# Q, K and V projections of a graph attention layer as 15 instead of 18 block products

## The chip, the cores and the metric

The kernel runs on one core of one Trainium2 chip. The metric is the device time of one execution in microseconds, as the median of several runs. The kernel before takes 3695.78 us (three runs, 3694.63 to 3697.33).

## The reference

For 128 graphs of 128 nodes and 768 features, everything in float32:

```python
h = jnp.maximum(_layernorm(x, axis=-1), 0.0)
q = _split_heads(h @ Wq + bq)      # 12 heads of 64
k = _split_heads(h @ Wk + bk)
v = _split_heads(h @ Wv + bv)
scores = jnp.einsum('bhqd,bhkd->bhqk', q, k) / jnp.sqrt(HD)
scores = scores + beta * adj_e
scores = jnp.where(adj_e > 0, scores, -9e15)
out = jnp.einsum('bhqk,bhkd->bhqd', softmax(scores), v)
x = x + out                        # heads joined again
```

## The kernel before

The function `direct` works on groups `G` of four graphs, 32 groups in all, so one group is a block of 512 rows. The 768 features are six chunks of 128 (`c` for the summed dimension, `oc` for the output dimension; an output chunk of 128 is two heads). The three weight matrices are loaded once, on the ACT queue, and stay in SBUF.

Per group: `load_x` brings x on the SP queue. `norm` (L125 to L138) normalises one graph: two `bn_stats` (L131), an aggregate and an add on DVE, a power on POOL (L137), and the scaling `xn` on DVE (L138). `to_hT` (L140 to L146) turns one feature chunk of the four graphs with four PE transposes `pt` and writes it through a ReLU on ACT as `hT`, 128 x 512. `make_bias` builds the transposed mask and bias from adj with DVE, POOL, four transposes `pb` and an ACT copy.

`project_qk(G, oc)` is 6 matmuls for q and 6 for k, each with 128x128 weights as the stationary operand and 512 columns of `hT` as the moving one, summed in one PSUM bank (`pwq`, `pwk`, L187); DVE reads q out (L191), ACT reads k out (L193). `project_v` takes `hT` as the stationary operand and 384 columns of `wv` as the moving one, 8 PSUM tiles of 6 matmuls (`pv`, L175), read out by DVE (L178). `scores` is 8 matmuls per output chunk (`sc`, L202), then a DVE operation (L207) and an exponential on ACT (L208) for each of two heads. `attend` is 8 matmuls (`av`, L217), and then sm, rs, seen, o and seen on DVE and an add into x on POOL (L229). The store of a whole group follows its last add.

In float32 each matmul is two records in the trace, each a weight load and a pass over the moving columns; "pass" below is one such record. A transpose is one.

The source order is: for each `oc`, `project_qk`, then (at `oc` 0) `project_v`, then `attend` of the chunk before, then `scores`; `norm` of the next group stands at `oc` 0 to 3, `to_hT` at 4 and 5. A planner puts each engine's instructions into a fixed order before the run: it follows source order where its own estimate says that an operand and a buffer are there, and takes something later in the source where they aren't. On the chip each engine runs its list in that order.

Of the kernel before, what the change touches and what calls it, by code (L numbers as in the profile page):

```python
# [59 lines left out]

@with_exitstack
def direct(ctx, tc, x, adj, wq, bq, wk, bk, wv, bv, beta, out, bad):

# [46 lines left out]
    bk_c = const.tile([P, NC], F32, name="bk_c")  # L110
    with nc.allow_non_contiguous_dma(reason="two biases of one row each"):
        nc.scalar.dma_start(bq_c, bq.rearrange("(c p) -> p c", p=P))
        nc.scalar.dma_start(bk_c, bk.rearrange("(c p) -> p c", p=P))
    bv_b = const.tile([P, D], F32, name="bv_b")
    nc.scalar.dma_start(bv_b, bv[None, :].to_broadcast([P, D]))
    w_sb = {}
    for name, src in (("wq", wq), ("wk", wk), ("wv", wv)):
        w_sb[name] = const.tile([P, NC, D], F32, name=name)
        for c in range(NC):
            nc.scalar.dma_start(w_sb[name][:, c, :], src[c * P:(c + 1) * P, :])  # L120
    vs = [const.tile([P, GRP, HEADS, VE], F32, name=f"v{i}") for i in range(2)]
    for v in vs:
        nc.gpsimd.memset(v[:, :, :, HD:VE], 1.0)

    def norm(G, g):  # L125
        if g == 0:
            xn[G] = big.tile([P, GRP, D], F32, tag="xn", name=f"xn_{G}", bufs=1)
        xg = xs[G][:, g, :]
        st = stat.tile([P, 2, nc.vector.BN_STATS_DIM], F32, tag="st", name=f"st_{G}_{g}")
        for s in range(2):  # L130
            nc.vector.bn_stats(st[:, s, :], xg[:, s * VH:(s + 1) * VH])  # L131
# [6 lines left out]
        nc.vector.tensor_scalar(xn[G][:, g, :], xg, mv[:, 0:1], rstd, op0=ALU.subtract, op1=ALU.mult)  # L138

    def to_hT(G, c):  # L140
        if c == 0:
            hT[G] = big.tile([P, NC, W], F32, tag="hT", name=f"hT_{G}")
        p = psum.tile([P, W], F32, tag="mm", name=f"pt_{G}_{c}", bufs=4)
        for g in range(GRP):
            nc.tensor.transpose(p[:, g * N:(g + 1) * N], xn[G][:, g, c * P:(c + 1) * P], ident)  # L145
        nc.scalar.activation(hT[G][:, c, :], p, AF.Relu)  # L146

    def make_bias(G):
        a = adjs[G]
        b = work.tile([P, GRP, N], F32, tag="b", name=f"b_{G}", bufs=1)  # L150
        nc.vector.tensor_scalar(b, a, beta_c, BIAS_CAP, op0=ALU.mult, op1=ALU.min)
        kp = work.tile([P, GRP, N], U8, tag="kp", name=f"kp_{G}", bufs=1)
        nc.vector.tensor_scalar(kp, a, 0.0, None, op0=ALU.is_gt)
        bm = stat.tile([P, GRP], F32, tag="bm", name=f"bm_{G}", bufs=1)
        b2 = work.tile([P, GRP, N], F32, tag="b2", name=f"b2_{G}", bufs=1)
        nc.gpsimd.tensor_tensor(b2, b, b, ALU.mult)
        nc.vector.tensor_reduce(bm, b2, AX.X, ALU.max)
        nc.vector.tensor_tensor(seen_b, seen_b, bm, ALU.max)
        nb = work.tile([P, GRP, N], F32, tag="nb", name=f"nb_{G}", bufs=1)
        nc.gpsimd.memset(nb, MASKED)  # L160
        nc.vector.copy_predicated(nb, kp, b)
        p = psum.tile([P, GRP, N], F32, tag="mm", name=f"pb_{G}", bufs=4)
        for g in range(GRP):
            nc.tensor.transpose(p[:, g, :], nb[:, g, :], ident)  # L164
        biasT[G] = big.tile([P, GRP, N], F32, tag="biasT", name=f"biasT_{G}")
        nc.scalar.copy(biasT[G], p)

    def project_v(G):
        v = vs[G % 2]
        HH = HEADS // 2  # L170
        for g in range(GRP):
            for s in range(2):
                p = psum.tile([P, VH], F32, tag="mm", name=f"pv_{G}_{g}_{s}", bufs=4)
                for c in range(NC):
                    nc.tensor.matmul(p, hT[G][:, c, g * N:(g + 1) * N],  # L175
                                     w_sb["wv"][:, c, s * VH:(s + 1) * VH],
                                     start=(c == 0), stop=(c == NC - 1))
                nc.vector.tensor_add(v[:, g, s * HH:(s + 1) * HH, 0:HD],  # L178
                                     p.rearrange("p (h d) -> p h d", d=HD),
                                     bv_b[:, s * VH:(s + 1) * VH].rearrange("p (h d) -> p h d", d=HD))  # L180

    def project_qk(G, oc):
        got = []
        for name in ("wq", "wk"):
            p = psum.tile([P, W], F32, tag="mm", name=f"p{name}_{G}_{oc}", bufs=4)
            for c in range(NC):
                nc.tensor.matmul(p, w_sb[name][:, c, oc * P:(oc + 1) * P], hT[G][:, c, :],  # L187
                                 start=(c == 0), stop=(c == NC - 1))
            t = work.tile([P, W], F32, tag=name, name=f"{name}T_{G}_{oc}", bufs=2)
            if name == "wq":  # L190
                nc.vector.tensor_scalar(t, p, bq_c[:, oc:oc + 1], SCALE, op0=ALU.add, op1=ALU.mult)  # L191
            else:
                nc.scalar.activation(t, p, AF.Identity, bias=bk_c[:, oc:oc + 1])  # L193
            got.append(t)
        return got

    def scores(G, oc, qT, kT):
        ps = [psum.tile([P, GRP, N], F32, tag="sc", name=f"sc_{G}_{oc}_{j}") for j in range(2)]
        for g in range(GRP):
            for j in range(2):  # L200
                r = slice(j * HD, (j + 1) * HD)
                nc.tensor.matmul(ps[j][:, g, :], kT[r, g * N:(g + 1) * N], qT[r, g * N:(g + 1) * N],  # L202
                                 start=True, stop=True)
        es = []
        for j in range(2):
            e = work.tile([P, GRP, N], F32, tag="e", name=f"e_{G}_{oc}_{j}")
            nc.vector.scalar_tensor_tensor(e, ps[j], SCORE_CAP, biasT[G], op0=ALU.min, op1=ALU.add)  # L207
            nc.scalar.activation(e, e, AF.Exp)  # L208
            es.append(e)
        return es  # L210

    def attend(G, oc, es):
        pa = psum.tile([P, 2, 512], F32, tag="av", name=f"av_{G}_{oc}", bufs=1)
        for g in range(GRP):
            for j in range(2):
                at = ((g % 2) * 2 + j) * VE
                nc.tensor.matmul(pa[:, g // 2, at:at + VE], es[j][:, g, :], vs[G % 2][:, g, 2 * oc + j, :],  # L217
                                 start=True, stop=True)
        got = pa[:, :, 0:4 * VE].rearrange("p a (b e) -> p a b e", e=VE)
        sm = stat.tile([P, 2, 4, 1], F32, tag="sm", name=f"sm_{G}_{oc}")  # L220
        nc.vector.tensor_scalar(sm, got[:, :, :, HD:VE], TINY, None, op0=ALU.max)  # L221
        rs = stat.tile([P, 2, 4, 1], F32, tag="rs", name=f"rs_{G}_{oc}")
        nc.vector.reciprocal(rs, sm)
        o = work.tile([P, 2, 4, HD], F32, tag="o", name=f"o_{G}_{oc}", bufs=2)
        nc.vector.tensor_mul(o, got[:, :, :, 0:HD], rs.to_broadcast([P, 2, 4, HD]))  # L225
        for i, t in enumerate((sm, rs)):
            nc.vector.tensor_tensor(seen[:, i, :], seen[:, i, :], t.rearrange("p a b e -> p (a b e)"), ALU.max)  # L227
        xo = xs[G][:, :, oc * P:(oc + 1) * P]
# [7 lines left out]
    for c in range(NC):  # L236
        to_hT(0, c)
# [3 lines left out]
    for G in range(NG):  # L241
        for oc in range(NC):
            qT, kT = project_qk(G, oc)
            if oc == 0:
                project_v(G)
# [158 lines left out]
```

## Time and profile before

| | us |
|---|---|
| median of three runs | 3695.78 |
| the profiled execution | 3694.58 |
| its span, from the first to the last instruction | 3692.5 |
| PE busy in it | 3648.3 |
| DVE busy | 1036.9 |
| ACT busy | 474.3 |
| POOL busy | 367.7 |

The busy time of an engine is the time in which at least one of its instructions runs. PE (matmul passes) and PEld (weight loads) are two rows of one engine, and run beside each other. A group of the steady part repeats every 113.85 us, so that the stretch between two `pv` of successive groups stands for all of them.

### The profile page before, as it was taken

How to read it: one execution, taken by the hardware profiler on the slowest of the kernel's cores; microseconds unless marked ns; L12 is line 12 of the kernel's file. 1: busy time of each engine (PE TensorE's matmuls, PEld its weight loads, DVE VectorE, ACT ScalarE, POOL GpSimd, SP SyncE). 2: the span in 40 equal slices, each digit the busy share in tenths (PEclk: the TensorE clock that was granted, in tenths of full speed). 3: DMA queues.
4: the chain of work that ended last, by engine and by line, in shares of the span. 5: the costliest groups of instructions: out<-in, count | busy, mean ns of one | idle time of the engine just before them, and what ended most of it. 6: DMA issues, size and time to landing. Idle time of an engine off the chain costs nothing.

```text
span 3692.5 us, 34646 instructions
## 1 busy us (share of the span) xinstructions
PE 3648.3 (99%) x14722; PEld 2100.4 (57%) x14722; DVE 1036.9 (28%) x2598; ACT 474.3 (13%) x801; POOL 367.7 (10%) x396
## 2 busy tenths in 40 slices
PE   6999999999999999999999999999999999999998
PEld 3555555555555555555555555555555555555554
DVE  3232222322222323223222232222332222322222
ACT  0111111111111101111101111111110111101111
POOL 1011000110001101011100011000110001100000
PEclk9999999999999999999999999999999999999999
DMA  4011010110101101001011011010110100100000
GB/s 144 3 38 38 34 38 3 38 38 35 38 3 38 38 35 38 21 21 38 35 37 38 3 38 38 35 38 3 38 38 35 38 17 24 38 35 35 18 1 35
DMA packets 55294, 118.80 MB, mean 32 GB/s; under 512 B 3552, under 2 KB 19936, under 8 KB 55136
## 3 DMA queue, kind: packets, MB, share of 16 engines
q1 hardware_dynamic: 50688, 109.06, 8.2%
q10 hardware_dynamic: 4448, 7.48, 0.6%
q8 instruction: 118, 1.93, 0.2%
q14 instruction: 40, 0.33, 0.0%
HBM read 66.20 MB, written 50.33 MB: 32 GB/s over the span
## 4 chain that ended last, share of the span: by engine, by line
PE 99%; DMA 1%; DVE 0%; ACT 0%; POOL 0%; issue 0%; ACTq 0%; DVEq 0%; POOLq 0%
PE pwq L187 27%; PE pv L175 27%; PE pwk L187 27%; PE av L217 9%; PE sc L202 6%; PE pt L145 3%; PE pb L164 0%; DMA adj<-in_adj_dram 0%; DMA x<-in_x_dram 0%; DVE xn L138 0%; POOL rstd L137 0%; DVE st L131 0%; DVE o L225 0%; ACT L146 0%; ACT e L208 0%
## 5 line engine op out<-in xcount | busy, mean ns | idle before, releaser
L187 PE MATMUL pwq<-hT,wq 128*128 128x512 f32 x2304 | 1033.9, 598 | 0.0
L187 PE MATMUL pwk<-hT,wk 128*128 128x512 f32 x2304 | 1020.1, 592 | 0.0
L175 PE MATMUL pv<-wv,hT 128*128 128x384 f32 x3072 | 996.0, 486 | 0.0
L175 PEld LDWEIGHTS pv<-wv,hT 128*128 128x128 f32 x3072 | 583.7, 190 | 413.9 <-issue 15.1
L187 PEld LDWEIGHTS pwk<-hT,wk 128*128 128x128 f32 x2304 | 437.8, 190 | 551.0 <-issue 543.4
L187 PEld LDWEIGHTS pwq<-hT,wq 128*128 128x128 f32 x2304 | 422.4, 190 | 474.9 <-issue 451.6
L229 POOL TENSOR_TENSOR x<-x,o 128x512 f32<-128x512 f32 x192 | 244.9, 1276 | 3125.7 <-DVE seen L227 3125.7
L178 DVE TENSOR_TENSOR v<-pv,bv_b 128x384 f32<-128x384 f32 x256 | 143.0, 559 | 1005.0 <-PE pv L175 1005.0
L217 PEld LDWEIGHTS av<-v,e 128*128 128x128 f32 x3072 | 373.2, 192 | 86.8 <-issue 76.5
L208 ACT ACTIVATE e<-e 128x512 f32<-128x512 f32 x384 | 231.2, 627 | 1382.5 <-DVE e L207 1381.6
L217 PE MATMUL av<-v,e 128*128 128x65 f32 x3072 | 364.2, 272 | 1.7 <-ACT e L208 1.7
L193 ACT ACTIVATE wkT<-pwk,bk_c 128x512 f32<-128x512 f32 x192 | 132.0, 687 | 1623.2 <-PE pwk L187 1623.2
L221 DVE TENSOR_SCALAR sm<-av 128x8 f32<-128x8 f32 x192 | 32.0, 167 | 1009.2 <-PE av L217 1009.2
L191 DVE TENSOR_SCALAR wqT<-pwq,bq_c 128x512 f32<-128x512 f32 x192 | 142.6, 743 | 526.9 <-PE pwq L187 526.9
L207 DVE SCALAR_TENSOR_TENSOR e<-sc,biasT 128x512 f32<-128x512 f32 x384 | 246.3, 683 | 0.8 <-PE sc L202 0.6
L202 PE MATMUL sc<-wqT,wkT 64*128 64x128 f32 x3072 | 223.1, 285 | 0.0
L202 PEld LDWEIGHTS sc<-wqT,wkT 64*128 64x128 f32 x3072 | 186.3, 187 | 13.5 <-issue 0.5
L131 DVE BATCH_NORM_STATS2 st<-x 128x6 f32<-128x384 f32 x256 | 132.0, 534 | 13.4 <-DMA x<-in_x_dram 13.1
L225 DVE TENSOR_TENSOR o<-av,rs 128x512 f32<-128x512 f32 x192 | 132.8, 692 | 9.4
L145 PE MATMUL pt<-ident,xn 128*128 128x128 f32 x768 | 101.2, 282 | 30.9 <-DVE xn L138 15.7
L146 ACT ACTIVATE hT<-pt 128x512 f32<-128x512 f32 x192 | 106.9, 595 | 165.2 <-PE pt L145 165.0
L145 PEld LDWEIGHTS pt<-ident,xn 128*128 128x128 f32 x768 | 84.5, 143 | 40.1 <-DVE xn L138 16.9
(37 smaller groups left out, 474.1 us busy)
## 6 DMA issues: line engine op xcount, KB each, us to landing
x<-in_x_dram SPq DMA_DIRECT2D x32, 1536.0 KB, 6.6
out_dram<-x SPq DMA_DIRECT2D x32, 1536.0 KB, 5.4
adj<-in_adj_dram SPq DMA_DIRECT2D x32, 256.0 KB, 2.8
wq<-in_L_gnn_Wq_dram ACTq DMA_DIRECT2D x6, 384.0 KB, 7.4
wk<-in_L_gnn_Wk_dram ACTq DMA_DIRECT2D x6, 384.0 KB, 10.4
wv<-in_L_gnn_Wv_dram ACTq DMA_DIRECT2D x6, 384.0 KB, 6.2
bv_b<-in_L_gnn_bv_dram ACTq DMA_DIRECT2D x1, 384.0 KB, 9.1
beta_c<-in_L_gnn_beta_dram ACTq DMA_DIRECT2D x1, 0.5 KB, 3.7
```

The costliest lines, as they stand in the source:

```text
L131: nc.vector.bn_stats(st[:, s, :], xg[:, s * VH:(s + 1) * VH])
L145: nc.tensor.transpose(p[:, g * N:(g + 1) * N], xn[G][:, g, c * P:(c + 1) * P], ident)
L175: nc.tensor.matmul(p, hT[G][:, c, g * N:(g + 1) * N], w_sb["wv"][:, c, s * VH:(s + 1) * VH], start=(c == 0), stop=(c == NC - 1))
L178: nc.vector.tensor_add(v[:, g, s * HH:(s + 1) * HH, 0:HD], p.rearrange("p (h d) -> p h d", d=HD), bv_b[:, s * VH:(s + 1) * VH].rearrange(" ...
L187: nc.tensor.matmul(p, w_sb[name][:, c, oc * P:(oc + 1) * P], hT[G][:, c, :], start=(c == 0), stop=(c == NC - 1))
L191: nc.vector.tensor_scalar(t, p, bq_c[:, oc:oc + 1], SCALE, op0=ALU.add, op1=ALU.mult)
L202: nc.tensor.matmul(ps[j][:, g, :], kT[r, g * N:(g + 1) * N], qT[r, g * N:(g + 1) * N], start=True, stop=True)
L207: nc.vector.scalar_tensor_tensor(e, ps[j], SCORE_CAP, biasT[G], op0=ALU.min, op1=ALU.add)
L208: nc.scalar.activation(e, e, AF.Exp)
L217: nc.tensor.matmul(pa[:, g // 2, at:at + VE], es[j][:, g, :], vs[G % 2][:, g, 2 * oc + j, :], start=True, stop=True)
L225: nc.vector.tensor_mul(o, got[:, :, :, 0:HD], rs.to_broadcast([P, 2, 4, HD]))
L229: nc.gpsimd.tensor_add(xo, xo, o.rearrange("p a (b j) d -> p (a b) (j d)", j=2))
```

## The change

The projections of a group become a product of block matrices. The activations are 2 x 3 blocks of 256 x 256 (two graphs each by two feature chunks, `A00` to `A12`), the weights 3 x 3 blocks of 256 x 256 (`B00` to `B22`); a "slice" of 768 output columns has six output blocks. There are three slices: `qk0` (q and k of the first three output chunks, side by side), `v`, and `qk1` (q and k of the last three). 18 block products would give a slice; the list `PRODUCTS` gives it with 15, each of one activation block or sum of blocks (`S..`) and one weight block or sum of blocks (`T..`).

A block product is 4 matmuls with 256 moving columns (before: 512 for q and k, 384 for v). Products of one chain (a, b, c or d) are added to the same PSUM bank, which always holds the running sum; after most products that sum is added to, or taken from, one output block in SBUF. In a qk slice the first use of each of the six output blocks is two ACT operations (one each for q and k, with the bias), the other ten are DVE operations of 128 x 512 from PSUM into SBUF; in the v slice all 16 are DVE operations. A chain's next product writes into the bank that the last use has to have read.

The sums of weight blocks are made once and stay in SBUF, 15 operations for each slice on DVE and POOL, from weights loaded block by block (for qk: 18 loads of 128 KB for each slice). The sums of activation blocks are 11 operations per group (7 on DVE, 4 on POOL), each with one buffer. The x tiles are loaded graph by graph and normalised in place; the x of the residual add is loaded a second time in pieces of 128 x 512 (`xo`), and the output is stored in such pieces. `attend` works in two halves. The scale of the scores moves into the exponential. `attention` and `slice_of` put scores and attend of half a group between the products of the slice after: the first half in `qk1` of the same group, the second in `qk0` of the next one. After the last slice the second half of the last group is left.

```diff
+PRODUCTS = (
+    ("S9", "T9", "c", (((1, 1), -1),)),
+    ("A10", "T12", "a", (((1, 0), -1),)),
+    ("S10", "T10", "b", (((1, 0), 1),)),
+    ("S2", "T2", "c", (((0, 1), -1),)),
+    ("S8", "B12", "d", (((1, 1), -1), ((1, 2), 1))),
+    ("S6", "T6", "a", (((0, 0), -1),)),
+    ("S3", "B01", "c", (((0, 2), -1),)),
+    ("S7", "T7", "b", (((0, 0), 1),)),
+    ("A12", "T4", "d", (((1, 0), -1),)),
+    ("S14", "B21", "c", (((0, 1), 1),)),
+    ("S0", "T0", "a", (((0, 2), 1),)),
+    ("A01", "T13", "b", (((0, 1), 1),)),
+    ("A02", "T1", "c", (((0, 0), 1),)),
+    ("S5", "B22", "a", (((1, 2), 1),)),
+    ("S11", "T11", "b", (((1, 1), 1),)),
+)
...
+    psum = ctx.enter_context(tc.tile_pool(name="psum", bufs=4, space=bass.MemoryType.PSUM))
...
+    def load_x(G, g):
+        xg[G, g] = work.tile([P, D], F32, tag="x", name=f"x_{G}_{g}")
+        nc.sync.dma_start(xg[G, g], x[G * GRP + g])
...
+    def sum_acts(G, n):
+        name, a, b, sign = SUMS_A[n]
+        t = work.tile([P, 2, H2], F32, tag=name, name=f"{name}_{G}", bufs=1)
+        e = nc.gpsimd if n % 3 == 1 else nc.vector
+        e.tensor_tensor(t, A[G, a], A[G, b], ALU.add if sign > 0 else ALU.subtract)
...
+    def product(G, sl, n):
+        an, bn, chain, uses = PRODUCTS[n]
+        first = all(p[2] != chain for p in PRODUCTS[:n])
+        if first:
+            banks[chain] = psum.tile([P, 2, H2], F32, tag="mm", name=f"p{chain}_{G}_{sl}")
+        p = banks[chain]
+        a, b = A[G, an], wt[sl, bn]
+        for i in range(2):
+            for c in range(2):
+                if sl == "v":
+                    lhs, rhs = a[:, c, i * N:(i + 1) * N], b[:, c, :]
+                else:
+                    lhs, rhs = b[:, c, i * P:(i + 1) * P], a[:, c, :]
+                nc.tensor.matmul(p[:, i, :], lhs, rhs, start=(first and i == 0 and c == 0), stop=(c == 1),
+                                 skip_group_check=True)
+        for (r, j), sign in uses:
...
+            elif key not in qk:
+                t = qk[key] = work.tile([P, 2, H2], F32, tag="qk", name=f"{sl}_{G}_{r}_{j}", bufs=10)
+                oc = j + 3 * int(sl[2])
+                for i in range(2):
+                    nc.scalar.activation(t[:, i, :], p[:, i, :], AF.Identity, bias=bqk[:, i, oc:oc + 1],
+                                         scale=float(sign))
+            else:
+                t = qk[key]
+                nc.vector.tensor_tensor(t, t, p, ALU.add if sign > 0 else ALU.subtract)
...
+    def attention(G, u):
+        todo = {}
+        for i in range(3):
+            todo.setdefault(1 + 4 * i, []).append(lambda oc=3 * u + i: scores(G, oc))
+            todo.setdefault(5 + 4 * i, []).insert(0, lambda oc=3 * u + i: attend(G, oc))
+        return todo
+
+    def slice_of(G, sl, todo):
+        for n in range(len(PRODUCTS)):
+            product(G, sl, n)
+            for f in todo.get(n, ()):
+                f()
...
     for G in range(NG):
+        todo = attention(G - 1, 1) if G else {}
+        if not G:
+            load_weights("v")
+            for n in range(len(SUMS_B)):
+                todo.setdefault(n, []).append(lambda n=n: sum_weights("v", n))
+        slice_of(G, "qk0", todo)
+        todo = {}
+        if not G:
+            load_weights("qk1")
+            for n in range(len(SUMS_B)):
+                todo.setdefault(n, []).append(lambda n=n: sum_weights("qk1", n))
+        if G + 1 < NG:
+            for g in range(GRP):
+                load_x(G + 1, g)
+                todo.setdefault(2 + 3 * g, []).append(lambda g=g: norm(G + 1, g))
+            todo.setdefault(8, []).append(lambda: make_bias(G + 1, load_adj(G + 1)))
+        slice_of(G, "v", todo)
+        todo = attention(G, 0)
+        if G + 1 < NG:
+            for i, (r, k) in enumerate(((0, 1), (1, 0), (1, 1), (1, 2), (0, 0), (0, 2))):
+                todo.setdefault((2, 3, 4, 6, 7, 8)[i], []).append(lambda r=r, k=k: to_hT(G + 1, r, k))
+            for n in range(len(SUMS_A)):
+                todo.setdefault(max(8, n + 4), []).append(lambda n=n: sum_acts(G + 1, n))
+        slice_of(G, "qk1", todo)
```

## Rows read from the trace of the kernel before

**Rows 1.** The page, parts 1 and 2: busy time of each engine; granted clock.

```profile
PE 3648.3 (99%) x14722; PEld 2100.4 (57%) x14722; DVE 1036.9 (28%) x2598; ACT 474.3 (13%) x801; POOL 367.7 (10%) x396
...
PEclk9999999999999999999999999999999999999999
```

**Rows 2.** The page, part 4: the chain that ended last, by line.

```profile
PE pwq L187 27%; PE pv L175 27%; PE pwk L187 27%; PE av L217 9%; PE sc L202 6%; PE pt L145 3%; PE pb L164 0%; DMA adj<-in_adj_dram 0%; DMA x<-in_x_dram 0%; DVE xn L138 0%; POOL rstd L137 0%; DVE st L131 0%; DVE o L225 0%; ACT L146 0%; ACT e L208 0%
```

**Rows 3.** Windows, one group: length, busy time by engine, clock, DMA share, GB/s.

```profile
1868.43:1982.28 113.85, 113.85 (x461) 65.56 (x460) 32.39 (x81) 14.76 (x25) 11.45 (x12) 1.00 0.09 31
```

**Rows 4.** Timeline of PE in one group: start, length, what, number of passes.

```profile
1856.77 1.53 PE L145 MATMUL pt<-ident,xn 128*128 128x128 f32 x12
1858.13 5.32 PE L187 MATMUL pwq<-hT,wq 128*128 128x512 f32 x12
1863.28 5.31 PE L187 MATMUL pwk<-hT,wk 128*128 128x512 f32 x12
1868.43 31.12 PE L175 MATMUL pv<-wv,hT 128*128 128x384 f32 x96
1899.39 1.90 PE L217 MATMUL av<-v,e 128*128 128x65 f32 x16
1901.22 1.16 PE L202 MATMUL sc<-wqT,wkT 64*128 64x128 f32 x16
1902.31 5.42 PE L187 MATMUL pwq<-hT,wq 128*128 128x512 f32 x12
1907.56 5.31 PE L187 MATMUL pwk<-hT,wk 128*128 128x512 f32 x12
```

**Rows 5.** The page, part 5: weight loads of `pv`, mean of one and idle between.

```profile
L175 PEld LDWEIGHTS pv<-wv,hT 128*128 128x128 f32 x3072 | 583.7, 190 | 413.9 <-issue 15.1
```

**Rows 6.** The page, part 5: DVE, ACT and POOL operations nearest to the new ones.

```profile
L229 POOL TENSOR_TENSOR x<-x,o 128x512 f32<-128x512 f32 x192 | 244.9, 1276 | 3125.7 <-DVE seen L227 3125.7
L178 DVE TENSOR_TENSOR v<-pv,bv_b 128x384 f32<-128x384 f32 x256 | 143.0, 559 | 1005.0 <-PE pv L175 1005.0
...
L193 ACT ACTIVATE wkT<-pwk,bk_c 128x512 f32<-128x512 f32 x192 | 132.0, 687 | 1623.2 <-PE pwk L187 1623.2
...
L191 DVE TENSOR_SCALAR wqT<-pwq,bq_c 128x512 f32<-128x512 f32 x192 | 142.6, 743 | 526.9 <-PE pwq L187 526.9
...
L225 DVE TENSOR_TENSOR o<-av,rs 128x512 f32<-128x512 f32 x192 | 132.8, 692 | 9.4
```

**Rows 7.** Timeline of DVE in the same group: one attend, scores, and a read-out.

```profile
1844.33 0.74 DVE L161 COPY_PREDICATED nb<-kp,b 128x512 f32<-128x512 uint8 x1 [1.10 <-POOL nb L160]
...
1855.78 0.17 DVE L221 TENSOR_SCALAR sm<-av 128x8 f32<-128x8 f32 x1 [6.13 <-PE av L217]
...
1856.93 1.29 DVE L207 SCALAR_TENSOR_TENSOR e<-sc,biasT 128x512 f32<-128x512 f32 x2
1858.33 2.45 DVE L138 TENSOR_SCALAR xn<-x,mv,rstd 128x768 f32<-128x768 f32 x4
1863.48 0.75 DVE L191 TENSOR_SCALAR wqT<-pwq,bq_c 128x512 f32<-128x512 f32 x1 [2.70 <-PE pwq L187]
```

**Rows 8.** Timeline of SP and DVE: load of x, and first statistics of it.

```profile
1909.20 0.37 SPq L88 DMA_DIRECT2D x<-in_x_dram  x1
...
1916.01 0.56 DVE L131 BATCH_NORM_STATS2 st<-x 128x6 f32<-128x384 f32 x1
```

**Rows 9.** Timeline of the start: ACT's first operation, PE's first projection.

```profile
33.46 1.28 ACT L146 ACT_TABLE_LOAD   x1 [33.46 <-DMA wv<-in_L_gnn_Wv_dram]
...
38.02 5.54 PE L187 MATMUL pwq<-hT,wq 128*128 128x512 f32 x12
```

**Rows 10.** Timeline of the end: PE waiting for the last exponentials.

```profile
3678.28 0.44 PE L217 MATMUL av<-v,e 128*128 128x65 f32 x2 [1.54 <-ACT e L208]
```

**Rows 11.** The page, part 6: stores and small loads, KB each, us to landing.

```profile
out_dram<-x SPq DMA_DIRECT2D x32, 1536.0 KB, 5.4
adj<-in_adj_dram SPq DMA_DIRECT2D x32, 256.0 KB, 2.8
```

More of the change, by code (lines that the diff above doesn't have):

```diff
@@ L137, in norm @@
         nc.gpsimd.tensor_tensor(rstd, ve, nhalf, ALU.pow)
[L138 to L151, printed above, removed]
+        nc.vector.tensor_scalar(t, t, mv[:, 0:1], rstd, op0=ALU.subtract, op1=ALU.mult)
+    def to_hT(G, r, k):
+        p = psum.tile([P, 2, 2, N], F32, tag="at", name=f"pt_{G}_{r}_{k}")
+        for c in range(2):
+            for g in range(2):
+                at = (2 * k + c) * P
+                nc.tensor.transpose(p[:, c, g, :], xg[G, 2 * r + g][:, at:at + P], ident)
+        t = work.tile([P, 2, H2], F32, tag="hT", name=f"hT_{G}_{r}_{k}", bufs=8)
+        nc.scalar.activation(t, p.rearrange("p c g n -> p c (g n)"), AF.Relu)
+        A[G, f"A{r}{k}"] = t
@@ L163, in make_bias @@
+        p = psum.tile([P, GRP, N], F32, tag="at", name=f"pb_{G}")
         for g in range(GRP):
             nc.tensor.transpose(p[:, g, :], nb[:, g, :], ident)
[L165 to L170, printed above, removed]
-        for g in range(GRP):
[L172 to L223, printed above, removed]
-        o = work.tile([P, 2, 4, HD], F32, tag="o", name=f"o_{G}_{oc}", bufs=2)
[L225 to L228, printed above, removed]
-        nc.gpsimd.tensor_add(xo, xo, o.rearrange("p a (b j) d -> p (a b) (j d)", j=2))
-        if oc == NC - 1:
-            nc.sync.dma_start(out[G * GRP:(G + 1) * GRP].rearrange("g n d -> n g d"), xs[G])
@@ new lines, in direct, with scores @@
+    es, xo = {}, {}
+    def scores(G, oc):
+        u, j = oc // 3, oc % 3
+        t = xo[G, oc] = work.tile([P, GRP, P], F32, tag="xo", name=f"xo_{G}_{oc}", bufs=3)
+        nc.sync.dma_start(t, x[G * GRP:(G + 1) * GRP, :, oc * P:(oc + 1) * P].rearrange("g n d -> n g d"))
+        ps = [psum.tile([P, GRP, N], F32, tag="at", name=f"sc_{G}_{oc}_{i}") for i in range(2)]
+        for g in range(GRP):
+            t = qk[G, f"qk{u}", g // 2, j]
+            at = slice((g % 2) * N, (g % 2 + 1) * N)
+            for i in range(2):
+                r = slice(i * HD, (i + 1) * HD)
+                nc.tensor.matmul(ps[i][:, g, :], t[r, 1, at], t[r, 0, at], start=True, stop=True)
+        for i in range(2):
+            e = es[G, oc, i] = work.tile([P, GRP, N], F32, tag="e", name=f"e_{G}_{oc}_{i}")
+            nc.vector.scalar_tensor_tensor(e, ps[i], SCORE_CAP * ISCALE, biasT[G], op0=ALU.min, op1=ALU.add)
+            nc.scalar.activation(e, e, AF.Exp, scale=1.0 / ISCALE)
@@ new lines, in attend @@
+    def attend(G, oc):
+        o = work.tile([P, 2, 4, HD], F32, tag="o", name=f"o_{G}_{oc}", bufs=2)
+        for r in range(2):
+            pa = psum.tile([P, 4, VE], F32, tag="at", name=f"av_{G}_{oc}_{r}")
+            for g in range(2):
+                for i in range(2):
+                    h = 2 * oc + i
+                    nc.tensor.matmul(pa[:, 2 * g + i, :], es[G, oc, i][:, 2 * r + g, :],
+                                     vt[G, "v", r, h // 4][:, 4 * g + h % 4, :], start=True, stop=True)
+            sm = stat.tile([P, 4, 1], F32, tag="sm", name=f"sm_{G}_{oc}_{r}")
+            nc.vector.tensor_scalar(sm, pa[:, :, HD:VE], TINY, None, op0=ALU.max)
+            rs = stat.tile([P, 4, 1], F32, tag="rs", name=f"rs_{G}_{oc}_{r}")
+            nc.vector.reciprocal(rs, sm)
+            nc.vector.tensor_mul(o[:, r], pa[:, :, 0:HD], rs.to_broadcast([P, 4, HD]))
+            for i, t in enumerate((sm, rs)):
+                s = seen[:, i, 4 * r:4 * r + 4]
+                nc.vector.tensor_tensor(s, s, t.rearrange("p b e -> p (b e)"), ALU.max)
+        t = xo[G, oc]
+        nc.gpsimd.tensor_add(t, t, o.rearrange("p a (b j) d -> p (a b) (j d)", j=2))
+        nc.sync.dma_start(out[G * GRP:(G + 1) * GRP, :, oc * P:(oc + 1) * P].rearrange("g n d -> n g d"), t)
@@ L234, in direct @@
+    def attention(G, u):
[9 more added lines that the diff above has]
+                f()
+    a = load_adj(0)
     for g in range(GRP):
         norm(0, g)
-    for c in range(NC):
-        to_hT(0, c)
@@ L238, in direct @@
-    make_bias(0)
-    prev = None
-    for G in range(NG):
[L242 to L245, printed above, removed]
-            if prev is not None:
-                attend(*prev)
-            prev = (G, oc, scores(G, oc, qT, kT))
-            if G + 1 < NG:
-                if oc < GRP:
-                    norm(G + 1, oc)
-                else:
-                    for c in range(3 * (oc - GRP), 3 * (oc - GRP) + 3):
-                        to_hT(G + 1, c)
-                if oc == 1:
-                    load_adj(G + 1)
-                if oc == 4:
-                    make_bias(G + 1)
-            if G + 2 < NG and oc == 1:
-                load_x(G + 2)
@@ L264, in direct @@
+    last = attention(NG - 1, 1)
+    for n in sorted(last):
+        for f in last[n]:
+            f()
+    worst = stat.tile([P, 3], F32, tag="worst", name="worst", bufs=1)
     nc.vector.tensor_reduce(worst[:, 0:2], seen, AX.X, ALU.max)
     nc.vector.tensor_reduce(worst[:, 2:3], seen_b, AX.X, ALU.max)
-    over = stat.tile([P, 3], F32, tag="over", name="over")
+    over = stat.tile([P, 3], F32, tag="over", name="over", bufs=1)
     nc.vector.tensor_scalar(over[:, 0:2], worst[:, 0:2], SUM_CAP, None, op0=ALU.is_gt)
```

134 lines of the change are left out of this document (91 added, 43 removed), and 7 rows, old and new, of tables (SUMS_A, SUMS_B).

## The prediction, made before the changed kernel was run

> **What bounds the kernel now.** [...] Busy PE alone proves little, so the chain that ended last comes next: by line it is all PE work, 81% of it the projections [rows 2]. Third, the window of one group: 113.85 us long, PE busy in all of it, DVE in 32.39, ACT in 14.76, POOL in 11.45 [rows 3]. So in the steady part nothing but PE ends a wait, and a us taken from PE's list is a us of time, as long as no other engine comes late. 32 x 113.85 = 3643 us of the span are such groups; some 38 us are start [rows 9] and some 11 us are end.
>
> **The cost of a pass.** What a projection costs is read from start to start, since the lengths overlap [rows 4]. 12 passes over 512 columns take 1863.28 - 1858.13 = 5.15 us, 0.4292 each; 96 passes over 384 columns take 1899.39 - 1868.43 = 30.96 us, 0.3225 each; 12 transposes of 128 columns take 1858.13 - 1856.77 = 1.36 us, 0.1133 each. The first two give 0.1067 us per 128 columns and 0.0024 on top. No row shows a pass over 256 columns: the line through 384 and 512 gives 0.2158, the one between 128 and 384 gives 0.2179. I take 0.2158, because the surplus at 128 columns can be a weight load that is just not hidden, and keep 0.2179 as the upper end: 360 x 32 x 0.0021 = 24 us.
>
> **What is removed and added on PE.** Per group, q and k are 6 x 2 x 6 matmuls, 144 passes: 61.80 us. v is 30.96 us. Together 92.76. The new form is 3 slices x 15 products x 4 matmuls x 2 passes = 360 passes of 256 columns: 77.69 us. That takes away 15.07 us per group, 482 us in 32 groups. Scores and attend keep their number of passes and columns, and so do the transposes. The transposes come in six pieces rather than two. A change of kind between neighbours can cost: 12 passes that begin after `sc` take 1907.56 - 1902.31 = 5.25 us and not 5.15 [rows 4]. Four more changes per group at 0 to 0.1 us are 0 to 13 us; I take 0, since the row after the transposes shows none.
>
> **Is each weight load still hidden?** There are 360 loads per group instead of 240, each behind 256 columns instead of 384 or 512. A load record of `pv` lasts 0.190 us and leaves 413.9 / 3072 = 0.135 us idle until the next [rows 5]; 0.190 fits into 0.2158. The better row is `pt`: each transpose loads a new 128 x 128 operand, and yet the pace is 0.1133; `av`, with 65 columns and a load per pass, has 1.83 / 16 = 0.114 [rows 4]. So a load needs no more than 0.114 us of its own and lies beside the pass before it. [...]
>
> **What is added on DVE.** A read-out of 128 x 512 from PSUM with a second input has its nearest rows in `o` (0.692), `v` with 384 columns (0.559) and `wqT` (0.743) [rows 6]; I take 0.69. Per group there are 10 + 10 + 16 = 36 of them: 24.8 us. Seven sums of activations, which no row shows with both inputs in SBUF on DVE, lie between 0.559 and 0.743 as well: 4.8 us. `attend` in halves: from sm to the next operation the five take 1856.93 - 1855.78 = 1.15 us [rows 7]; a half saves only the columns of `o`, 256 x (0.692 - 0.559) / 128 = 0.27 us, so two halves take 1.76, 0.6 more, 3.7 us in six. Removed: 6 x 0.743 and 8 x 0.559, 9.0 us. DVE goes from 32.4 to 56.7 us of a group of 98.8. ACT loses 6 x 0.687 and gets 24 operations of 256 columns, each between half of 0.687 and all of it; at 0.45, 10.8 us: 21.5. POOL gets 4 sums at up to 1.276: 16.6. By busy share none of them is near PE.
>
> **The new wait.** A chain's next product must wait for the read-out of the one before, and PE runs in order, so all of PE's list stands behind it. Within a slice the same chain comes back after at least two other products, 2 x 8 x 0.2158 = 3.45 us. A read-out begins 0.2 us after PE (`wqT` at 1863.48, the next matmul at 1863.28 [rows 7, 4]) and takes 0.69, so DVE may be late by 2.5 us before PE feels it. In the qk slices DVE has only 20 of the 32 read-outs of a group; attend and scores put 1.76 + 1.29 = 3.1 us at a time between them, and PE itself needs 1.83 + 1.09 = 2.9 us for these [rows 4]. In the v slice PE has 15 x 1.73 = 25.9 us and nothing else, DVE 16 x 0.69 = 11.0. Norms and bias are what remains of rows 3: 32.4 - 9.0 - 6 x (1.15 + 1.29) = 8.8 us; in source order they stand there too, with hand-offs to POOL of about 1 us each [rows 7], four for norms and two for the bias. Walked through in source order, product 8 ends at 15.5 us; then read-out (16.4), norm (1.7 + 1, 19.1), bias (2 + 2, 23.1), read-out of product 9 at 23.8; product 12 of the same chain could have started at 20.7. That is 3.1 us per group, the upper end. The lower end is 0, because the planner doesn't keep source order: the load of x at 1909.20 and its statistics at 1916.01 [rows 8] belong to a norm that stands in the next group's loop, and the four `xn` follow the last transposes at once [rows 7]. In the new kernel x tiles come free with the transposes in `qk1` of the group before, so norms can run in the gaps of the qk slices. I take 0.8 us per group, nearer to 0: 26 us, with 0 and 99 as ends.
>
> **DMA.** SP issues 17 transfers per group instead of 3, and x is read twice: 4.9 MB in 98.8 us, 50 GB/s, where 31 GB/s keep the DMA engines 9% busy [rows 3]. POOL's add waits for `xo`, which is asked for with the scores, some ten us ahead; 256 KB land in 2.8 us [rows 11]. Hidden; without that cover a late x would hold DVE in the norm, and then PE.
>
> **Start and end.** PE's first projection waits until 38.02 because ACT issues weight loads until 33.46 [rows 9]. The first slice needs a third of them, but sums besides, and the sums for the first two slices (27 on DVE at 0.69, 19 us) and the buffers shared by weight blocks and q, k are in the way in the first group. I take 0, with -18 and +15 as ends. At the end PE waited 1.5 us for exponentials [rows 10]; three attends are left now instead of two, but the last store is 256 KB instead of 1536, landing in 2.8 rather than 5.4 us [rows 11]: +1 us, within -1 and +3.
>
> **The sum.** 3692.5 - 482 + 26 + 0 + 1 = 3237 us of span; the profiled run has 2.1 us around its span and lies 1.2 below the median: 3240 us.
>
> **The rivals.** (1) *DVE comes late in every group.* The planner puts norm, bias or sums ahead of read-outs, or DVE stands in line behind x or POOL, and PE loses more than the walked 3.1 us, say 4.5 to 8: 3214 + 32 x 4.5 to 8 gives 3358 to 3470, in the middle 3410. For it: DVE's load almost doubles, and in the v slice 11.0 + 8.8 + 6 hand-offs of 1 would fill 25.8 of 25.9 us. Against it: rows 8. (2) *The weight load sets the pace, and the kernel is slower.* The change has 15.07 / 360 = 0.042 us to give away per pass; if a 256-column pass takes over 0.258 us, it loses. With a load of 0.114 wholly outside, 32 x 360 x 0.114 = 1313 us are added: 4550 us. For it: half as much time behind each load as with q and k. Against it: `pt` at 0.1133. (3) *The start shrinks more*, or passes overlap better, to below 3195: the loads before the first product are a third of before. That the form saves nothing can be excluded by counting: 360 passes are in the source.
>
> **How the numbers follow.** Forecast 81%, rival 1 12%, rival 2 4%, rival 3 3%. The range takes in the ends: 3240 - 26 - 18 - 1 = 3195 below; above, 3240 + 73 + 24 + 13 + 15 would be 3365 with all at their worst, and I stop at 3355. A measurement of this kernel tells about 0.2%, 7 us, from no change; faster is the forecast, rivals 1 and 3, 96%, of which I leave 1% to a pace near the 0.258: faster 95%, same 1%, slower 4%.
>
> **What would show it.** Eight passes of a product start to start in 1.73 us, a group of 98.8 us plus stalls from `v` to `v`; idle PE ahead of products put down to DVE read-outs, 0.8 us per group; DVE near 57 us per group; the clock unchanged. Wrong if product passes are spaced over 0.22 us, if PE's idle time exceeds 3 us per group, or if the first product comes outside 20 to 53 us.

## The result

The changed kernel takes 3228.69 us (median of 4 runs, 3228.16 to 3229.05). Against the kernel before, run beside it, the ratio is 0.8734, 95% interval 0.8719 to 0.8749: 12.7% less time. 3240 us were predicted, 3195 to 3355 as the range. Its profiled execution has a span of 3227.2 us, 465 less than before.

The page of the changed kernel, parts 1, 2 and 4, answers to [rows 1] and [rows 2]: busy time by engine, the granted clock in 40 slices, and the chain that ended last.

```profile
PE 3185.1 (99%) x18562; PEld 2821.5 (87%) x18562; DVE 1777.4 (55%) x4516; ACT 677.1 (21%) x1377; POOL 546.4 (17%) x544
...
PEclk9999999999999999999999999999999999999998
...
PE 97%; DVE 1%; DMA 0%; POOL 0%; issue 0%; ACT 0%; ACTq 0%; POOLq 0%; DVEq 0%
```

PE still has nearly all of the chain, with less to do; DVE's busy share has doubled, from 28% to 55%, and DVE is on the chain with 1%. One group, from the bias transposes of one v slice to those of the next, as a window (length, busy time of PE, PEld, DVE, ACT and POOL, clock, DMA share, GB/s), answers to [rows 3]:

```profile
1666.30:1765.31 99.01, 99.01 (x581) 87.81 (x580) 54.41 (x140) 21.11 (x43) 16.30 (x16) 1.00 0.17 51
```

A group takes 99.01 us instead of 113.85, PE busy in all of it; DVE has 54.4 us of work, ACT 21.1, POOL 16.3. PE's timeline in the v slice of that group (start, length, what, passes) answers to [rows 4]:

```profile
1652.49 1.89 PE L257 MATMUL pa_v<-v_T,hT 128*128 128x256 f32 x8
1654.22 1.89 PE L257 MATMUL pb_v<-v_T,S 128*128 128x256 f32 x8
1655.94 1.89 PE L257 MATMUL pc_v<-v_T,S 128*128 128x256 f32 x8
1657.67 1.89 PE L257 MATMUL pd_v<-v_B,S 128*128 128x256 f32 x8
1659.39 1.89 PE L257 MATMUL pa_v<-v_T,S 128*128 128x256 f32 x8
1661.12 1.89 PE L257 MATMUL pc_v<-v_B,S 128*128 128x256 f32 x8
1662.85 1.89 PE L257 MATMUL pb_v<-v_T,S 128*128 128x256 f32 x8
1664.58 1.89 PE L257 MATMUL pd_v<-v_T,hT 128*128 128x256 f32 x8
1666.30 0.60 PE L236 MATMUL pb<-ident,nb 128*128 128x128 f32 x4
```

The products start 1.726 us apart ((1666.30 - 1652.49) / 8), 0.2158 us per pass, in source order and with no idle time. DVE's timeline beside it shows the read-outs:

```profile
1654.42 0.69 DVE L268 TENSOR_TENSOR v<-bv_b,pa_v 128x512 f32<-128x512 f32 x1 [1.04 <-PE pa_v L257]
1656.14 0.69 DVE L273 TENSOR_TENSOR v<-v,pb_v 128x512 f32<-128x512 f32 x1 [1.04 <-PE pb_v L257]
```

Each begins 0.2 us after its product and takes 0.69; DVE then waits 1.04 us for PE. No norm stands in this slice: the planner has moved the norms behind the transposes, from about the tenth product of `qk1` on. The bias of a later group stays in the v slice, in pieces between the read-outs of its second half. DVE's timeline, one line of a norm, one of the bias and the read-out behind it:

```profile
1606.92 0.75 DVE L199 TENSOR_SCALAR x<-x,mv,rstd 128x768 f32<-128x768 f32 x1
...
1669.36 0.73 DVE L233 COPY_PREDICATED nb<-kp,adj 128x512 f32<-128x512 uint8 x1 [0.42 <-POOL nb L232]
1669.99 0.67 DVE L273 TENSOR_TENSOR v<-v,pc_v 128x512 f32<-128x512 f32 x1
```

The last line reads out a product of chain c that ended at 1668.47. It begins 1.3 us later than a read-out that has DVE to itself, and PE doesn't feel it: the chain's next product starts on time at 1671.92.

Where PE still waits is seen in its list of waits (what waited for what, us in total, times, longest):

```profile
PE pt L206 <- DVE x L199: 16.4, 2, 13.1
PE pb L236 <- DVE nb L233: 5.8, 1, 5.8
PE av L309 <- ACT e L300: 4.5, 3, 1.5
PE pc_qk L257 <- DVE S L215: 2.9, 1, 2.9
PE pf L386 <- DVE over L383: 2.6, 1, 2.6
```

None of these comes 32 times. They belong to the start and the end.

### The profile page after: what moved, and what is told of

The parts are those of the page before. It is cut to its first block, busy times and chain, and to the rows that moved or that the text cites. A ratio compares the mean times of both kernels' runs of the same rounds, so it can differ in the third digit from the quotient of the medians.

```text
span 3227.2 us, 46121 instructions
## 1 busy us (share of the span) xinstructions
PE 3185.1 (99%) x18562; PEld 2821.5 (87%) x18562; DVE 1777.4 (55%) x4516; ACT 677.1 (21%) x1377; POOL 546.4 (17%) x544
## 3 DMA queue, kind: packets, MB, share of 16 engines
q1 hardware_dynamic: 238080, 159.42, 16.6%
## 4 chain that ended last, share of the span: by engine, by line
PE 97%; DVE 1%; DMA 0%; POOL 0%; issue 0%; ACT 0%; ACTq 0%; POOLq 0%; DVEq 0%
PE pc_qk L257 17%; PE pb_qk L257 14%; PE pa_qk L257 14%; PE av L309 10%; PE pc_v L257 8%; PE pb_v L257 7%; PE pd_qk L257 7%; PE pa_v L257 7%; PE sc L296 7%; PE pd_v L257 3%; PE pt L206 3%; PE pb L236 0%; DMA qk_B<-in_L_gnn_Wk_dram 0%; DVE qk_T L176 0%; DVE v_T L176 0%
## 5 line engine op out<-in xcount | busy, mean ns | idle before, releaser
L320 POOL TENSOR_TENSOR xo<-xo,o 128x512 f32<-128x512 f32 x192 | 244.2, 1272 | 1722.5 <-DVE seen L318 1371.2
L257 PE MATMUL pb_qk<-S,qk_T 128*128 128x256 f32 x1536 | 373.1, 386 | 0.0
L257 PEld LDWEIGHTS pb_qk<-S,qk_T 128*128 128x128 f32 x1536 | 279.3, 190 | 39.4 <-issue 0.3
L257 PE MATMUL pa_qk<-S,qk_T 128*128 128x256 f32 x1024 | 248.6, 386 | 0.0
L257 PE MATMUL pc_qk<-S,qk_B 128*128 128x256 f32 x1024 | 248.6, 386 | 0.0
L257 PE MATMUL pc_qk<-S,qk_T 128*128 128x256 f32 x1024 | 245.0, 383 | 2.9 <-DVE S L215 2.9
L296 PE MATMUL sc<-qk 64*128 64x128 f32 x3072 | 225.7, 286 | 0.0
L257 PEld LDWEIGHTS pc_qk<-S,qk_T 128*128 128x128 f32 x1024 | 194.0, 192 | 28.8 <-DVE S L215 3.3
L296 PEld LDWEIGHTS sc<-qk 64*128 64x128 f32 x3072 | 188.1, 188 | 30.2 <-issue 21.2
L257 PEld LDWEIGHTS pa_qk<-S,qk_T 128*128 128x128 f32 x1024 | 186.9, 190 | 29.2
```

The lines of the kernel that those rows point to most:

```text
L257: nc.tensor.matmul(p[:, i, :], lhs, rhs, start=(first and i == 0 and c == 0), stop=(c == 1), skip_group_check=True)
L296: nc.tensor.matmul(ps[i][:, g, :], t[r, 1, at], t[r, 0, at], start=True, stop=True)
L320: nc.gpsimd.tensor_add(t, t, o.rearrange("p a (b j) d -> p (a b) (j d)", j=2))
```

## Experiments

The theory: PE's passes are the time, at a pace that holds each weight load inside the pass, and the read-outs have room to spare because two products lie between two of a chain and because the planner spreads the rest of DVE's work. The rivals: the gain has other sources than the three products less; DVE is close to its limit; the weight load is close to setting the pace.

### The ordinary 18 products in the same frame

```diff
-PRODUCTS = ( ... 15 products ... )
-SUMS_A = ( ... )
-SUMS_B = ( ... )
+PRODUCTS = tuple((f"A{r}{k}", f"B{k}{j}", f"{r}{j}", (((r, j), 1),) if k == 2 else ())
+                 for r in range(2) for j in range(3) for k in range(3))
+SUMS_A = ()
+SUMS_B = ()
```

(`hT` has 12 buffers here, since no sums stand in for it.)

> The frame of the changed kernel, but with the ordinary 18 block products: each of the six output blocks of a slice is the sum of three products in one PSUM bank, read once at its end (ACT in the qk slices, DVE in v), and no sums of blocks are made. Theory (PE's passes are the time): 18 x 4 x 2 x 3 = 432 passes of 256 columns instead of 360, at 0.2158 us 93.2 us instead of 77.7 per group: 15.5 us more in each of 32 groups, 497 us, less some 10 us of the start that the sums no longer hold up: 3715 us, within 3700 and 3730, slower than the kernel before although DVE has 30 read-outs and sums less per group. Rival (the gain came from the other edits, such as the split x loads, ACT's read-outs and the halves of attend): it stays below 3500 us.

3711.19 us, ratio to the kernel before 1.0038 (1.0024 to 1.0052). PE's timeline in its v slice, 72 passes on each side of the bias transposes:

```profile
1660.64 15.70 PE L232 MATMUL p_v<-v_B,hT 128*128 128x256 f32 x72
1676.18 0.60 PE L211 MATMUL pb<-ident,nb 128*128 128x128 f32 x4
1676.62 15.71 PE L232 MATMUL p_v<-v_B,hT 128*128 128x256 f32 x72
1692.16 3.62 PE L232 MATMUL p_qk<-hT,qk_B 128*128 128x256 f32 x16
...
1790.73 0.60 PE L211 MATMUL pb<-ident,nb 128*128 128x128 f32 x4
```

72 passes in 15.54 us are 0.2158 each, the pace of the changed kernel. A group takes 1790.73 - 1676.18 = 114.55 us, and 114.55 - 99.01 = 15.54: in the steady part the whole gain is the 72 passes less per group, and the other edits bring nothing there. Against the kernel before, such a group is 0.70 us longer; 432 passes of 256 columns (93.2 us) in place of 240 wider ones (92.8) are 0.47 of that. The run as a whole is 14.4 us slower than the kernel before on the same chip (3711.19 against 3696.81), where 32 x 0.70 would be 22.4, so the frame also moves start and end. The first product comes earlier, at 24.38 instead of 38.02:

```profile
24.38 32.74 PE L232 MATMUL p_qk<-hT,qk_B 128*128 128x256 f32 x144
```

Its end has three waits of 1.5 us for exponentials instead of one, as the changed kernel's has.

### Each bank read twice, and three times

```diff
+    junk = const.tile([P, W], F32, name="junk")
...
+                for _ in range(1):      # 2 in the second kernel
+                    nc.vector.tensor_scalar(junk, p.rearrange("p g w -> p (g w)"), 1.0, None, op0=ALU.mult)
                 nc.vector.tensor_tensor(t, t, p, ALU.add if sign > 0 else ALU.subtract)
```

The same stands ahead of the 16 read-outs in the v slice.

> Ahead of each of the 36 read-outs on DVE per group, DVE reads the same bank once more into a tile that nobody uses. Theory (a read-out has 2.5 us to spare, and DVE has room): DVE goes from 55 to some 80 us of the 99 us group, a chain's read-out takes 1.6 us instead of 0.9 against the 3.45 us that two products leave, and PE loses under 1 us per group: 3229 to 3261 us. Rival 1 (DVE is already at the edge in the v slice, where 16 read-outs of 0.69 us would become 22 us of 25.9): PE waits 5 us or more in every group, 3390 us or more.

> The same with two more readings ahead of each read-out on DVE: some 50 us more DVE work per group, 105 us against 99 us of PE, and 3 x 0.69 + 0.2 = 2.3 us from a product's end to the end of its read-out. Theory (DVE's room is 99 - 55 = 44 us per group and then it is the bound): at least 6 us more per group, 3420 us or more, up to 3620 since DVE also waits for others. If PE alone decided, whatever DVE does: 3229 us.

Read twice: 3225.36 us, ratio 0.8723 (0.8709 to 0.8738), the same as the changed kernel within the intervals. Read three times: 3375.93 us, ratio 0.9131 (0.9116 to 0.9146). One group of each as a window, columns as above:

```profile
1567.42:1666.43 99.01, 99.01 (x581) 87.81 (x580) 75.50 (x176) 21.11 (x43) 16.38 (x16) 1.00 0.17 51
```

```profile
1628.31:1731.70 103.39, 101.32 (x581) 87.62 (x580) 95.53 (x213) 20.82 (x43) 16.36 (x16) 1.00 0.17 49
```

With 75.5 us of DVE work the group still takes 99.01 us, to the hundredth. With 95.5 it takes 103.39, and PE now waits for DVE, in every group:

```profile
PE pd_v L258 <- DVE v L271: 55.1, 32, 2.6
...
PE pb_v L258 <- DVE v L276: 6.6, 30, 0.5
```

So rival 1 was far away: DVE could take 21 us more per group. Where the limit lies was expected too far to the slow side (3420 us or more): a second reading of a bank adds (75.50 - 54.41) / 36 = 0.59 us and not 0.69, because the records of operations that follow each other at once on DVE overlap by about 0.1 us. The limit isn't met in DVE's sum over a group, 95.5 of 103.4 us, but in one stage: the waits that come in nearly every group are all those of v products for v read-outs. 16 read-outs of 0.69 + 2 x 0.59 us are 29.9 us in a v slice whose products take PE 25.9. That the 4.0 us between them are near the 4.38 us that the group is longer is no proof of the size: the planner has rearranged this slice, with scores, transposes and first products of `qk1` between those of v, and bias work between DVE's read-outs. (The list shows only part of this: records of successive products overlap, 1.89 us long at 1.726 from start to start in the changed kernel, and a wait inside the overlap counts as busy PE; the distance from group to group shows all of it.)

### Passes of 128 columns

```diff
-                nc.tensor.matmul(p[:, i, :], lhs, rhs, start=(first and i == 0 and c == 0), stop=(c == 1),
-                                 skip_group_check=True)
+                for h in range(2):
+                    w = slice(h * P, (h + 1) * P)
+                    nc.tensor.matmul(p[:, i, w], lhs, rhs[:, w], start=(first and i + c + h == 0), stop=(c == 1),
+                                     skip_group_check=True)
```

> Every matmul of a product is cut into two of 128 moving columns: 720 passes per group with a weight load each, the same products. Theory (a load lies beside the pass before it and needs up to 0.114 us): a pass has the pace of the transposes, 0.1133 us, 81.6 instead of 77.7 us per group, 3.9 us more: 3354 us, within 3330 and 3375. [...]

3314.09 us, ratio 0.8962 (0.8947 to 0.8977); a little below the expected 3330 to 3375. PE's timeline:

```profile
1704.50 1.95 PE L259 MATMUL pa_v<-v_T,S 128*128 128x128 f32 x16
1706.28 1.95 PE L259 MATMUL pc_v<-v_B,S 128*128 128x128 f32 x16
1708.07 1.95 PE L259 MATMUL pb_v<-v_T,S 128*128 128x128 f32 x16
1709.86 1.95 PE L259 MATMUL pd_v<-v_T,hT 128*128 128x128 f32 x16
```

16 passes take 1.787 us, 0.1117 each, each with its own weight load. That is 0.0050 over the 0.1067 that 128 columns take by themselves, against 0.0024 at 384 and 512. A load is thus hidden even behind 128 columns, all but 0.003 us of it at most. 720 x 0.1117 = 80.4 us per group, 2.7 more than 77.7, and the group takes 101.68 instead of 99.01. Rival 2 falls: with a load of 0.114 us, the pace of `av` [rows 4], outside the pass, a pass would take an estimated 0.1067 + 0.114 = 0.22 us and the 720 passes 158 us, where the whole group takes 101.68. In such a group, as a window, PEld is busy beside PE in 100.44 of these:

```profile
1609.96:1711.64 101.68, 101.68 (x942) 100.44 (x941) 54.38 (x140) 21.23 (x43) 16.35 (x16) 1.00 0.17 50
```

### Norms and bias tied to their places

```diff
+    def pin(t, G, n):
+        (r, j), _ = PRODUCTS[n][3][0]
+        nc.vector.scalar_tensor_tensor(t[:, 0:1], vt[G, "v", r, j][:, 0, 0:1], 0.0, t[:, 0:1],
+                                       op0=ALU.mult, op1=ALU.add)
     def norm(G, g):
         t = xg[G, g]
+        if G:
+            pin(t, G - 1, 2 + 3 * g)
...
     def make_bias(G, a):
+        if G:
+            pin(a.rearrange("p g k -> p (g k)"), G - 1, 8)
```

> The norms and the bias of the next group are tied to their places in the source: before each, DVE writes one column of its input with a sum that needs the v block read out just before (times zero), so they can't begin until products 2, 5, 8 and 11 of the v slice are read. Theory (the planner's spreading of this work over the qk slices is what keeps PE from waiting): DVE has 11 + 9 us and six hand-offs to POOL inside the 25.9 us of the v slice, and PE loses between 0 and the walked 3.1 us per group; I expect 1.5, 3277 us. If the spreading doesn't matter: 3229 us, within 5.

3270.19 us, ratio 0.8845 (0.8831 to 0.8858): 41.5 us more than the changed kernel, 1.3 per group. The size was as expected, the place was not. PE's waits, and PE's timeline in one group:

```profile
PE pb L245 <- DVE nb L242: 42.9, 32, 5.6
...
1695.24 0.66 PE L245 MATMUL pb<-ident,nb 128*128 128x128 f32 x4 [1.21 <-DVE nb L242]
```

(One of the 32 waits, of 5.6 us, is that of the first group, which isn't tied.) Not a chain waits but the bias transposes, which stand in PE's list ahead of products and now get their mask late. The read-outs of the v slice are in time even so: the planner puts them between the pieces of the norms and the bias. On DVE, a read-out between a norm's aggregate and its add:

```profile
1684.71 0.19 DVE L201 BATCH_NORM_AGGREGATE mv<-st 128x2 f32<-128x12 f32 x1
1684.82 0.63 DVE L277 TENSOR_TENSOR v<-bv_b,pc_v 128x512 f32<-128x512 f32 x1
1685.37 0.15 DVE L203 TENSOR_SCALAR ve<-mv 128x1 f32<-128x1 f32 x1
```

The walk in source order (3.1 us at product 12) took a norm and a bias for blocks that nothing comes into.

### One product between two of a chain

```diff
-    S9 c, A10 a, S10 b, S2 c, S8 d, S6 a, S3 c, S7 b, A12 d, S14 c, S0 a, A01 b, A02 c, S5 a, S11 b
+    S9 c, A10 a, S2 c, S6 a, S3 c, S0 a, S14 c, S10 b, A02 c, S7 b, S8 d, A01 b, A12 d, S11 b, S5 a
```

(The lines of `PRODUCTS` in another order, named here by activation and chain.)

> The same 15 products in another order, in which only one product lies between two of a chain (c a c a c a c b c b d b d b a): 1.73 us from the end of one to the start of the next instead of 3.45. Theory (the read-out needs 0.2 + 0.69 us, so 0.8 us stay to be late): read-outs that stand behind an attend and scores on DVE (3.1 us) make PE wait, some 0.3 to 1 us at each of six places: 2 to 6 us per group, 3293 to 3421 us. If the spacing doesn't matter because DVE is never late: 3229 us.

3276.07 us, ratio 0.8864 (0.8851 to 0.8878): 47 us more, 1.5 per group, below the expected 2 to 6. PE's waits of the steady part, and those of the group that begins with `pb` at 1694.13 (the one before it takes 1694.13 - 1593.59 = 100.54 us, from `pb` to `pb`):

```profile
PE pd_qk L257 <- ACT qk L278: 15.0, 28, 0.7
PE pb_v L257 <- DVE v L273: 10.8, 30, 0.4
...
1698.54 1.99 PE L257 MATMUL pb_v<-v_T,hT 128*128 128x256 f32 x8 [0.36 <-DVE v L273]
...
1738.63 1.99 PE L257 MATMUL pd_qk<-hT,qk_T 128*128 128x256 f32 x8 [0.50 <-ACT qk L278]
```

With one product between, chains do wait, in nearly every group. The wait of `pb_v` stands beside the bias work on DVE, which makes read-outs of the v slice late. The wait of `pd_qk` is put down to ACT, but begins on DVE, as the bank is read by both in turn:

```profile
1736.97 0.67 DVE L282 TENSOR_TENSOR qk<-qk,pd_qk 128x512 f32<-128x512 f32 x1
...
1737.74 0.84 ACT L278 ACTIVATE qk<-pd_qk,bqk 128x256 f32<-128x256 f32 x2 [1.69 <-DVE ve L196]
```

(What released the last line is inferred, and named as `ve`; DVE's read-out of the same bank had ended 0.1 us before.) The product before it in that chain had ended by 1734.51; until 1736.97 DVE was busy with scores, pieces of a norm and a sum. One reason why chains wait less than thought can be read here too: an attend stands on PE (1736.24 to 1738.06) between the two products of that chain, besides the one product. The two products of the change are thus more than was needed on average, and enough everywhere.

### End and start

```diff
-            e = es[G, oc, i] = work.tile([P, GRP, N], F32, tag="e", name=f"e_{G}_{oc}_{i}")
+            e = es[G, oc, i] = work.tile([P, GRP, N], F32, tag="e", name=f"e_{G}_{oc}_{i}", bufs=5)
...
-        slice_of(G, "qk1", todo)
-    last = attention(NG - 1, 1)
-    for n in sorted(last):
-        for f in last[n]:
-            f()
+        if G + 1 == NG:
+            todo.setdefault(12, []).append(lambda: scores(G, 3))
+            todo.setdefault(14, []).append(lambda: scores(G, 5))
+        slice_of(G, "qk1", todo)
+    attend(NG - 1, 3)
+    scores(NG - 1, 4)
+    attend(NG - 1, 5)
+    attend(NG - 1, 4)
```

(The fifth buffer of `e` holds for all groups; a group still takes 1665.61 - 1566.60 = 99.01 us from `pb` to `pb`.)

> Only the end is changed: in the last group the scores of chunk 3 stand behind product 12 and those of chunk 5 behind product 14, as soon as their blocks are finished, and attend 3, scores 4, attend 5, attend 4 follow. Theory (after the last product PE waits three times 1.5 us for exponentials, and the granted clock falls to 0.5, so its passes take twice as long): two waits go and fewer passes run at half clock, 6 to 10 us less, 3220 us. If the end is set by DVE, POOL and the store behind PE: 2 us or less.

In the second kernel besides:

```diff
-    make_bias(0, a)
...
+        if not G:
+            todo.setdefault(4, []).insert(0, lambda: make_bias(0, a))
         slice_of(G, "v", todo)
```

> The same, and the bias of the first group is made in its v slice, not ahead of the first products: PE no longer stands behind its transposes (a wait of 5.8 us, with some 1.2 us lost to the lower clock after it). Theory: 6 to 9 us less than with the end alone, 3212 us. If PE then waits for the sums of activations or weights in the same place: no gain over the end alone.

The end alone: 3217.85 us, ratio 0.8704 (0.8692 to 0.8716), below the interval of the changed kernel; the 10.8 us that it takes off are a little more than the expected 6 to 10. End and start: 3215.30 us, ratio 0.8696 (0.8684 to 0.8707); on the same chip 2.6 us less than the end alone (3215.05 to 3215.75 against 3216.70 to 3218.83). It is the fastest of all. Windows of the end, first three of the changed kernel (up to the end of its last product, from the end of the first wait, from the end of the second), then one with the new end (the granted clock is the third value from the right):

```profile
3180.00:3196.90 16.90, 16.90 (x105) 14.99 (x103) 9.15 (x29) 1.23 (x2) 1.69 (x2) 1.00 0.16 48
3199.57:3203.60 4.03, 4.03 (x20) 3.65 (x20) 0.39 (x3) 0.54 (x1) 0.00 (x0) 0.58 0.24 69
3206.80:3218.20 11.40, 9.85 (x48) 8.90 (x48) 3.26 (x16) 1.76 (x3) 1.26 (x1) 0.50 0.16 46
```

```profile
3195.63:3205.22 9.59, 9.59 (x90) 8.79 (x89) 7.34 (x35) 2.39 (x4) 2.80 (x3) 1.00 0.28 82
```

In the changed kernel PE waits three times 1.5 us for exponentials after its last product. Behind the first of these waits the granted clock is 0.58, and behind the second 0.50: 48 passes of attend and scores take 9.85 us, where 90, eight of them a whole product, take 9.59 with the new end, which has no such wait and a clock of 1.00. The start gave 2.6 us, less than the expected 6 to 9. The wait of 5.8 us for the bias transposes is gone, but waits for read-outs (`qk`) come in its place; the wait for `S` was there before, with 2.9 us:

```profile
PE pb_qk L257 <- DVE qk L282: 4.9, 3, 2.5
PE pc_qk L257 <- DVE S L215: 3.2, 1, 3.2
PE pc_qk L257 <- DVE qk L282: 1.3, 1, 1.3
```

Read-outs of the first slice stand in DVE's list behind sums of weight blocks: the bias was one piece of a DVE queue, and PE now waits for the rest of it.

## Why the prediction was right, step by step

**PE as the bound.** Right: 99.01 us of PE in a group of 99.01. The 18 products in the same frame put a price on it: they are 482 us slower, where 72 x 0.2158 x 32 = 497 us of passes are more, and the 15 us between are close to what the start costs less without sums: the first product comes 3.1 us earlier (24.38 against 27.50), and most of the 12 us that the first group loses (below) aren't lost.

**The pass of 256 columns.** 0.2158 was taken from the line through 384 and 512, and 0.2158 it is. The upper end, 0.2179, came from the transposes; the products cut into passes of 128 columns have 0.0026 of the transposes' 0.0042 us over the line through 384 and 512, so the surplus does belong to the short pass. That it is the load, as assumed, isn't shown by itself. A group was put at 98.78 and takes 99.01: the other 0.23 are changes of kind between neighbours: a product ahead of scores takes 1.82 us from start to start (1579.82 to 1581.64), one behind them 1.83 (1582.73 to 1584.56), where others take 1.73. The prediction held this term at 0, within 0 to 13 us; it is 7.

**Weight loads.** Right, and rival 2 was further away than its 4% say: the rows of `pt` and `av` [rows 4] had the answer.

**DVE, ACT, POOL, DMA.** DVE 56.7 predicted, 54.4 measured; ACT 21.5 and 21.1, with a read-out of 256 columns at 0.470 us where 0.45 was taken; POOL 16.6 and 16.3; DMA 50 and 51 GB/s. DVE's sum was 4% high because lengths of neighbours were added that overlap by about 0.1 us.

**Stalls.** This term was mis-sized: 0.8 us per group, 26 us in all, were taken; the chains wait in no group of the steady part, so the sign named for it, idle PE ahead of products in each group, didn't come; the 0.23 us of the paragraph on the pass are 7 us in all. The step that failed is the walk through the v slice in source order. It treated norm and bias as blocks and allowed for the planner only by a value between the ends. The trace shows the norms in the qk slices, and the bias in the v slice in pieces that make a read-out at most 1.3 us late, where 2.5 can be spared; the tied norms show that even in their places they do not hold up a chain.

**Start and end.** +1 us was predicted for both together; it is about +9. The start was put at 0 and comes out near it, at +1, by luck in part, as two large differences nearly cancel. The first product comes earlier by 10.5 us, at 27.50 instead of 38.02 and inside the stated -18 to +15:

```profile
27.50 3.78 PE L257 MATMUL pc_qk<-S,qk_T 128*128 128x256 f32 x8 [2.94 <-DVE S L215]
```

But the first group loses some 12 us to its sums, the bias and slow first passes. From the first product to the end of the last there are 3169.3 us, where 32 x 99.01 less what this stretch doesn't have (three attends and three scores behind it, 8.8 us, and the first transposes of x ahead of it, 2.6) would be 3156.9; the same account of the kernel before, with two attends and one scores behind its last projection, comes out at +0.5. The end is the second term that was mis-sized: it costs some 8 us more, outside the stated -1 to +3. Behind the last product there are 30.4 us, 8.8 of them attends and scores at the steady pace, against 18.7 and 4.7 us in the kernel before. The prediction took over the one wait of 1.5 us of the kernel before; there are three, and passes at half clock behind them, for which it had no term.

**The sum.** 3692.5 - 482.2 + 7.4 + 9 is 3226.7, where the span is 3227.2. The forecast was 10 us too high because the stalls were put 19 us too high and start and end 8 us too low; two errors of opposite sign left a small one.

## What to carry to other kernels

Where one engine is busy throughout and its pace per unit is read from start to start, a saving in its units is a saving in time (here 72 passes of 0.2158 us, 15.54 us of a group), and an unmeasured size can be estimated from the line through its neighbours (here 0.2158 us for 256 columns; at 128 columns the line was 0.0026 us too low). A new wait is sized by the time between two uses of the same buffer less the reader's delay and length, and what else the reader's engine has to do counted here only in so far as it couldn't be put elsewhere or between the reads. When a steady part is well understood, the error lies in start and end: list there which engine is late, and whether the clock holds.

## What was not expected of the hardware

In the kernel before, a wait of 1.54 us of PE near the end [rows 10], with 3.05 us of PE work in the 4.50 us up to its end and 1.22 in the last 2.67 of them, left the clock nearly untouched (0.94 in the next 2.6 us). In the changed kernel a wait of 1.50 us, with 1.17 us of PE work in the 2.67 us up to its end, is followed by 0.58 and then 0.50 to the end. So the length of one wait doesn't tell what the clock does after it; with the waits taken away it stayed at 1.00. Windows up to the end of the wait and behind it, of the kernel before:

```profile
3673.70:3678.20 4.50, 3.05 (x33) 2.72 (x31) 2.37 (x7) 1.29 (x2) 1.23 (x1) 1.00 0.00 0
3678.20:3680.80 2.60, 2.26 (x16) 1.94 (x16) 0.06 (x1) 0.63 (x2) 0.05 (x1) 0.94 0.00 0
```

Eight passes of the first product take 3.57 us (27.50 to 31.07), 0.446 each, twice the 0.2158 of the steady part, though the granted clock of that stretch is shown as 1.00. In the kernel with the changed start they take 3.40 us, and there the column shows 0.53. So at the very start that column alone doesn't tell the length of a pass; whether the clock was down there in the changed kernel too stays open.
